# Two graph layers on one core: one exponential over two neighbouring weight tiles in the encoder, and another split of its row sums

## The chip, the cores and the metric

The kernel runs on one core of one Trainium2 chip. The metric is the device time of one execution in microseconds (us). The times below are of whole executions, the profile is of one execution.

## What is computed

The input is `x` (4096 nodes, 512 features) and a 0/1 matrix `adj` of 4096 by 4096. Two layers follow each other: a graph attention autoencoder (encoder attention, a small network, decoder attention with the same weights, a small network), and a second, different graph attention. The change is in the encoder attention alone. Cut to it, the reference is:

```
f1 = einsum('hnd,hd->hn', Xw, V[:, 0]);  f2 = einsum('hnd,hd->hn', Xw, V[:, 1])   # h: 4 heads
sig = sigmoid(f1[:, :, None] + f2[:, None, :])
att = softmax of sig over those j with adj[i, j] != 0, and 0 elsewhere
Xa  = einsum('hij,hjd->hid', att, Xw)
```

A sigmoid is half of a tanh plus a constant, and a constant falls out of a softmax. So the weight of a pair is exp(0.5 · tanh(0.5 · (f1 + f2))) times the mask `adj`; a row's output is the weighted sum of `Xw`, divided by the sum of its weights (the denominator).

## The kernel before, in words

**Blocks and tiles.** `attention` (called for the encoder with the name "enc") goes over eight blocks: four heads, each with two halves of 2048 target nodes. In a block it goes over 32 tiles j of 128 source nodes. A weight tile `e` has 128 partitions (sources) and 2048 columns (targets) of float32, 1 MB. Below, blocks are counted from 1 to 8 and tiles from 0 to 31.

**One tile.** `tanh_weights` makes it: ScalarE takes the tanh of the row `rowb` plus a per-partition score (L571), then the exp in place (L572), and VectorE multiplies by the mask `a` (L573), which SyncE's queue loads from HBM (L213, five buffers). TensorE then multiplies it with the values in four matmuls of 512 columns (L470, for the fourth bank at the block's start L467), into four PSUM banks.

**Denominators.** Each tile must also be added to its block's row sums, in one of three ways. The list `ENC` says how from the fourth block on:

```
ENC = (0, 2, 5, 7, 10, 12, 15, 17, 20, 22, 25), (8, 9, 30, 31)
```

Tiles of the first list are added to `acc2` by transfers: GpSimd's queue issues two per tile, one for each half of the columns, 512 KB each, that add to what is there (L490; the first of a block is a plain copy). Since all of them add to the same tile, each waits for the one before it on its half. Tiles of the second list are multiplied with ones on TensorE (L268). All others are added to `acc` by VectorE (L498, L500). At the end of a block TensorE sums `acc2` and `acc` with ones as well. The first transfer of the next block, which overwrites `acc2`, waits for that.

**Slots.** Weight tiles lie in a ring of eight: `EP` = 2 in the pool `keep`, which the decoder uses too, and 6 in the pool `spool`. Tile j+8 takes the place of tile j, so its tanh waits until everything that reads tile j has ended: the multiply, the matmuls, the transfers of the sum, and for every fifth tile (4, 9, 14, ...) a store to HBM for the decoder (`ekeep`, SyncE's queue, L439).

**A block's ending** runs inside the next block: VectorE copies the banks out (L683) and the denominators (L274), GpSimd's queue sends these to HBM, back as a column (L280), the inverses to HBM (L288), and spread over all partitions (`rb`, L293); VectorE multiplies the output by them (L687) and takes statistics (L690).

**Order.** Each engine works through its own list in order. A scheduler fixes these lists when the program is built, from the order of the code and its own estimates. A wait therefore holds up all that is behind it on its engine. In the lists of before, ScalarE has in the encoder two tanhs, then their two exps, then the next two tanhs.

Of the kernel before, what the change touches and what calls it, by code (L numbers as in the profile page):

```python
# [31 lines left out]
FP = mybir.dt.float32  # L32
U8 = mybir.dt.uint8
AF = mybir.ActivationFunctionType
ALU = mybir.AluOpType
# [4 lines left out]
N, F, H, D, P = 4096, 512, 4, 128, 128  # L40
IB = 512
NIB = N // IB
NJ = N // P
C = IB // P

TB = 2048
NTB = N // TB
SB = TB // IB
# [8 lines left out]
TINY = 1e-30  # L57
# [4 lines left out]
ENC_FIRST = (), (5, 6, 11, 12, 17, 18, 24, 25, 30, 31)  # L62
ENC_SECOND = (12, 14, 17, 19, 22, 24, 26), (1, 2, 4, 5, 7, 8, 30, 31)
ENC_THIRD = (0, 3, 6, 9, 12, 15, 18, 21, 24), (7, 8, 16, 30, 31)
ENC = (0, 2, 5, 7, 10, 12, 15, 17, 20, 22, 25), (8, 9, 30, 31)

GAT_FIRST = (0, 2, 4, 6, 8, 10, 12, 14, 16, 18, 20, 22, 24), (30, 31)
GAT = tuple(range(3, 28, 2)), (31,), True
# [5 lines left out]
EP = 2  # L74

EVICT = 2
INVERT = 4

HB = TB // 2
HD = D // 2  # L80
# [10 lines left out]
def kernel(ctx, tc, x, xT, adjT, w0, w0T, v0, wencT, wdecT, vecs, w1, w1T, a1, outT):  # L91
    nc = tc.nc
# [46 lines left out]
    score = consts.tile([P, 2, NTB, H, NJ // NTB], FP, name="score")  # L139

    def column(t, j, h):
        j = j % (NJ // NTB), j // (NJ // NTB)
        return t[:, j[1], h, j[0]:j[0] + 1]
# [10 lines left out]
    bias = consts.tile([P, C], FP, name="bias")  # L154
# [68 lines left out]

    def attention(what, keep, pools, weights, values, row_of, out, finish, ebufs, modes=None, invert=None,
                  kept=None, sums=None, sums2=None, extras={}, row0=None, masks0=(), in_parts0=1,
                  finish_last=None, behind=(), fast=None):

# [18 lines left out]


        spool, made, masks0 = pools, 0, list(masks0)  # L250
        if invert is not None:
            acc = spool.tile([P, TB], FP, name="acc") if sums is None else sums
            sums2 = (spool.tile([P, TB], FP, name="acc2"), None) if sums2 is None else sums2

        def weight_tile():
            nonlocal made
            made += 1
            if (made - 1) % (EP + ebufs) < EP:
                return keep.tile([P, TB], FP, name="e", tag="ek", bufs=EP)
            return spool.tile([P, TB], FP, name="e", bufs=ebufs)  # L260


        hop = nc.scalar if kept is None else nc.gpsimd
# [129 lines left out]
        later, last_ones, last_main, products_of = {}, None, None, ()  # L393
        rowb = row0 if row0 is not None else next_row_of(0, 0)
        blocks = [(h, tb) for h in range(H) for tb in range(NTB)]
        for n, (h, tb) in enumerate(blocks):
# [14 lines left out]
            for j in range(NJ):  # L411
# [4 lines left out]
                with pinned([a_load, *products_of, last_main] if j else []):  # L416
                    if (n, j) in extras:
                        extras[n, j](a_load)
                    if not last and j == NJ - 10:
                        next_row = next_row_of(*blocks[n + 1])  # L420
                e = weight_tile()
                store = j % KEEP == KEEP - 1 and kept is not None
                if store and kept == "read":
                    a_load = nc.sync.dma_start(e, ekeep[h][tb][j // KEEP])
                else:
                    if masks0:
                        a, a_load = masks0.pop(0)
                    else:
                        a = mask_tile(keep)
                        a_load = load_mask(a, tb, j)  # L430

                    with pinned([*(products_of[:1] if kept == "read" and n == 0 and j < 8 else ()),
                                 *(behind if n == 0 and j < EP else ())]):
                        products_of = weights(e, rowb, a, j, h, SB if NJ * n + j < in_parts0 else 1)


                    if stores and (store if n > 1 else j % KEEP == KEEP - 3):
                        k, t = stores.pop()
                        (nc.sync if n > 1 else nc.scalar).dma_start(ekeep[h][tb][k], t)  # L439
                    if store:  # L440
                        stores.append((j // KEEP, e))
# [3 lines left out]
                elif j - 1 in pairs:  # L445
                    made_sums = sums_second(sums_of, e1, e)
                    products_of = products_of[0], made_sums
# [75 lines left out]
            if not last:  # L523
# [5 lines left out]
                rowb = next_row  # L529
# [39 lines left out]
    def tanh_weights(e, rowb, a, j, h, parts):  # L569
# [3 lines left out]
            last_dve = nc.vector.tensor_mul(e, e, a)  # L573
        return last_act, last_dve

    a_att, b_att, a_mlp, b_mlp = (coefs[:, k, :] for k in range(4))

    with tc.tile_pool(name="keep", bufs=1) as keep:

        with tc.tile_pool(name="f_small", bufs=1) as small, tc.tile_pool(name="f_work", bufs=2) as work:  # L580
            xs = []
# [4 lines left out]
            for ib in range(NIB):  # L586
# [7 lines left out]
                for c in range(0, C, 1 if ib == 0 else C):  # L594
                    n = 1 if ib == 0 else C
# [11 lines left out]
            for ib in range(NIB):  # L607
# [45 lines left out]
                for c in range(C):  # L653
                    j = ib * C + c
# [12 lines left out]
                if ib == SB - 1:  # L667
                    store_rows(rows[0], targets(0))
                    row0 = keep.tile([P, TB], FP, name="rowb", bufs=2)
                    row0_load = load_row(row0, rows[0], 0)  # L670
                    with tc.issue_after(row0_load.ins):
                        masks0 = []
# [48 lines left out]
        with tc.tile_pool(name="enc", bufs=1) as spool:  # L721

            with tc.issue_after(last_copy.ins), tc.issue_after(masks0[-1][1].ins):
                attention("enc", keep, spool, tanh_weights, R[0:4], lambda h, tb: (rows[tb], h), out_enc,
                          (scaled, statistics), 6, lambda n: (ENC_FIRST, ENC_SECOND, ENC_THIRD, ENC)[min(n, 3)],
                          (TINY, ALU.max), "write", row0=row0, masks0=masks0,
                          extras={(2, 8): encoder_weights, (H * NTB - 1, 10): coefs_of_three,
                                  (H * NTB - 1, 12): bias_of_three, (H * NTB - 1, 20): scale_three})

# [43 lines left out]
        with tc.tile_pool(name="m_small", bufs=1) as small, tc.tile_pool(name="m_work", bufs=3) as work:  # L773
# [8 lines left out]
            behind_it = []  # L782
# [54 lines left out]

        with tc.tile_pool(name="dec", bufs=1) as spool:
            attention("dec", keep, spool, tanh_weights, xc, lambda h, tb: (rows[tb], h), out_dec, (scaled, elu), 5,
                      kept="read", behind=behind_it, fast=(z, xd, stationaries),  # L840
                      extras={(H * NTB - 1, 28): decoder_weights})


# [284 lines left out]
```

## Time and profile before

| what | us |
|---|---|
| median of 3 runs (lowest, highest) | 3199.43 (3197.14, 3202.03) |
| the profiled execution, its own time | 3198.86 |
| its span, first to last instruction | 3197.1 |
| one encoder block of 32 tiles (blocks 5, 6, 7) | 118.19, 118.18, 118.19 |
| ScalarE busy in such a block | 118.2 |
| VectorE busy in such a block | 114.3 |
| TensorE busy in such a block | 116.6 |

The profile's busy times are of one execution. A line of a timeline gives the start, the length, the engine, the line of the kernel, what is written and read, how many instructions are taken together, and in brackets how long the engine had been idle and what ended that. Instructions that follow each other directly overlap a little in the records, so a step from start to start is shorter than a length. Matmuls are pipelined and their ends are modelled, so TensorE's busy share overstates its work.

### The profile page before, as it was taken

The page shows a single profiled execution, that of the slowest core. Times are in us where ns is not written, and L with a number is a line of the kernel's source. Part 1 is how long each engine was busy: PE and PEld are TensorE (multiplying, and loading weights), DVE is VectorE, ACT ScalarE, POOL GpSimd, SP SyncE. Part 2 cuts the span into 40 slices and gives each one's busy share as a digit, 9 for nine tenths or more (in the row PEclk, how much of TensorE's full clock was granted, in tenths as well). Part 3 has the DMA queues.
Part 4 walks back from the last instruction along what each step waited for, and adds up shares of the span by engine and source line. Part 5 has one row for each costly group of instructions (what it writes and reads, how often), then busy time and mean ns, then how long its engine had stood idle before and what let it go on. Part 6 is the DMA issues. An engine that isn't in the chain of part 4 may idle for free.

```text
span 3197.1 us, 30054 instructions
## 1 busy us (share of the span) xinstructions
PE 3146.9 (98%) x10539; PEld 1371.7 (43%) x10539; DVE 2938.7 (92%) x2222; ACT 2573.7 (81%) x1825; POOL 525.9 (16%) x680
## 2 busy tenths in 40 slices
PE   7999999999999999999999999999999999999998
PEld 6334444444444463333333333458544444444443
DVE  7989999999999678999999999685699999999998
ACT  7999999999998449999999999466755665666663
POOL 3001211211211000010100100026312222222221
PEclk9999999999999999999999999999999999999999
DMA  9998978988987014444445454322579999899996
GB/s 212 198 194 253 267 209 233 271 223 229 267 227 190 7 44 148 155 159 156 160 162 165 141 168 145 97 105 74 149 193 228 219 219 243 217 213 229 236 213 156
DMA packets 214792, 589.25 MB, mean 184 GB/s; under 512 B 25872, under 2 KB 28976, under 8 KB 198640
## 3 DMA queue, kind: packets, MB, share of 16 engines
q0 software_dynamic: 71008, 231.95, 37.9%
q1 hardware_dynamic: 132200, 332.53, 30.1%
q10 hardware_dynamic: 11432, 22.85, 2.0%
q8 instruction: 83, 1.36, 0.2%
q14 instruction: 69, 0.57, 0.1%
HBM read 378.15 MB, written 84.30 MB: 145 GB/s over the span
## 4 chain that ended last, share of the span: by engine, by line
PE 68%; DVE 15%; issue 8%; ACT 5%; DMA 3%; DVEq 0%; ACTq 0%; POOL 0%; POOLq 0%; SPq 0%
PE ps L470 28%; PE ps L332 22%; PE ps L739 7%; DVE e L573 5%; DVE acc L500 4%; PE den L332 3%; PE ps L950 3%; ACT e L571 3%; DMA a<-mask 3%; DVE R L500 2%; ACT e L572 2%; DVE e L1045 2%; PE den L268 1%; PE ps L799 1%; PE ps L658 1%
## 5 line engine op out<-in xcount | busy, mean ns | idle before, releaser
L470 PE MATMUL ps<-e,R 128*128 128x512 f32 x3992 | 1737.9, 595 | 19.2 <-DVE e L573 16.6
L470 PEld LDWEIGHTS ps<-e,R 128*128 128x128 f32 x3992 | 754.6, 190 | 998.8 <-issue 921.6
L573 DVE TENSOR_TENSOR e<-e,a 128x2048 f32<-128x2048 f32 (+1 forms) x470 | 1049.5, 2261 | 80.2 <-ACT e L572 66.9
L571 ACT ACTIVATE e<-rowb,score 128x2048 f32<-128x2048 f32 (+1 forms) x470 | 909.1, 1969 | 20.3 <-PE ps L332 8.9
L572 ACT ACTIVATE e<-e 128x2048 f32<-128x2048 f32 (+1 forms) x470 | 866.9, 1879 | 4.4 <-DVE e L573 0.7
L332 PE MATMUL ps<-e,R 128*64 128x512 f32 x2624 | 746.8, 592 | 1.6 <-DVE e L573 1.5
L1044 ACT ACTIVATE e<-rowb,nq,jcol 128x2048 f32<-128x2048 f32 x224 | 459.6, 2088 | 263.3 <-DMA w<-e 133.1
L1045 DVE SCALAR_TENSOR_TENSOR e<-e,jcol,a 128x2048 f32<-128x2048 f32 (+1 forms) x265 | 592.9, 2271 | 2.8 <-ACT e L1044 2.8
L332 PEld LDWEIGHTS ps<-e,R 128*64 128x64 f32 x2624 | 241.9, 137 | 319.7 <-issue 316.2
L500 DVE TENSOR_TENSOR R<-R,e 128x2048 f32<-128x2048 f32 x128 | 292.5, 2285 | 0.0
L500 DVE TENSOR_TENSOR acc<-acc,e 128x2048 f32<-128x2048 f32 x122 | 278.7, 2284 | 1.0
L490 POOL DMA_DIRECT2D w<-e x178 | 151.9, 865 | 605.8 <-DMA w<-e 293.1
L739 PE MATMUL ps<-R,w 128*128 128x512 f32 x512 | 220.4, 592 | 0.6 <-DVE w L697 0.6
L490 POOL DMA_DIRECT2D acc<-e x142 | 119.1, 893 | 521.3 <-DMA acc<-e 238.4
L739 PEld LDWEIGHTS ps<-R,w 128*128 128x128 f32 x512 | 97.1, 190 | 123.0 <-issue 117.7
L332 PE MATMUL den<-e,R 128*64 128x512 f32 x320 | 149.8, 592 | 0.0
L332 PE MATMUL ps<-e,w 128*64 128x512 f32 x288 | 138.1, 592 | 0.7 <-DVE e L573 0.7
L293 POOL DMA_DIRECT2D rb<-rinvs x60 | 34.5, 578 | 520.7 <-DVE R L687 449.4
L950 PE MATMUL ps<-w1x,hT 128*128 128x260 f32 x512 | 115.5, 384 | 1.4 <-ACT hT L928 1.4
L332 PE MATMUL ps<-t,w 128*64 128x512 f32 x336 | 111.3, 592 | 1.1 <-DVE t L341 1.1
L950 PEld LDWEIGHTS ps<-w1x,hT 128*128 128x128 f32 x512 | 96.5, 190 | 19.9 <-issue 3.4
L332 PE MATMUL ps<-t,R 128*64 128x512 f32 x192 | 90.2, 592 | 0.0
(209 smaller groups left out, 2115.5 us busy)
## 6 DMA issues: line engine op xcount, KB each, us to landing
a<-mask SPq DMA_DIRECT2D x720, 256.0 KB, 4.3
w<-e POOLq DMA_DIRECT2D x178, 512.0 KB, 6.8
acc<-e POOLq DMA_DIRECT2D x142, 512.0 KB, 7.1
e<-ekeep SPq DMA_DIRECT2D x48, 1024.0 KB, 5.1
ekeep<-e SPq DMA_DIRECT2D x36, 1024.0 KB, 7.1
mask<-in_adjT POOLq DMA_DIRECT2D x8, 2048.0 KB, 105.0
rowb<-rows SPq DMA_DIRECT2D x16, 1024.0 KB, 5.5
rb<-rinvs POOLq DMA_DIRECT2D x60, 256.0 KB, 4.7
```

The costliest lines, as they stand in the source:

```text
L293: hop.dma_start(rb, everywhere(rinvs[h][tb], 0, s * IB, IB))
L332: last_half = nc.tensor.matmul(b[g * HD:(g + 1) * HD, :], weight, x, start=start, stop=stop)
L470: last_main = nc.tensor.matmul(b, block(values[h], j), e[:, s * IB:(s + 1) * IB], start=(j == 0), stop=(j == NJ - 1))
L490: nc.gpsimd.dma_start(into_half, e_half, **({"accum_op": ALU.add} if j > moved[0] else {}))
L500: nc.vector.tensor_add(acc, acc, e)
L571: nc.scalar.activation(e, rowb, AF.Tanh, bias=column(score[:, 1], j, h), scale=0.5)
L572: last_act = nc.scalar.activation(e, e, AF.Exp, scale=0.5)
L573: last_dve = nc.vector.tensor_mul(e, e, a)
L739: last = nc.tensor.matmul(z, w[:, fb, o * P:(o + 1) * P], nodes(src[fb], ib), start=(fb == 0), stop=(fb == C - 1))
L950: m = nc.tensor.matmul(banks[k][:, 0:2 * DX], hT[:, fb, c * P:(c + 1) * P], w1x[:, fb, 2 * k:2 * k + 2, :].rearrange("p h x -> p (h x)"), ...
L1044: last_act = nc.scalar.activation(e, rowb, AF.Relu, bias=column(nq, j, h), scale=column(jcol, j, h))
L1045: last_dve = nc.vector.scalar_tensor_tensor(e, e, column(jcol2, j, h), a, ALU.add, ALU.mult)
```

## The change

From the fourth block on (`PAIRS_FROM = 3`, counted from 0), ScalarE makes two neighbouring tiles with three instructions: two tanhs as before, and one exp over both tiles, 4096 columns. For that the two tiles must lie side by side, so the ring's slots become slices of two persistent tiles (`ring` with 2 slots, `er` with 6). The decoder takes its two shared slots from the same `ring`. The multiply by the mask stays one instruction per tile, and both multiplies of a pair now need the pair's exp.

The list of the row sums changes as well: twelve tiles instead of eleven go by transfers, three instead of four by ones; VectorE's share stays at 17 tiles.

```diff
-ENC = (0, 2, 5, 7, 10, 12, 15, 17, 20, 22, 25), (8, 9, 30, 31)
+ENC = (0, 2, 4, 6, 8, 10, 13, 15, 17, 20, 22, 24), (12, 30, 31)
...
+PAIRS_FROM = 3
...
+        ring2 = spool.tile([P, ebufs, TB], FP, name="er") if by_pairs is not None else None
...
+        def slots_of_two():
+            nonlocal made
+            k = made % (EP + ebufs)
+            made += 2
+            return ring[:, k:k + 2, :] if k < EP else ring2[:, k - EP:k - EP + 2, :]
...
-                e = weight_tile()
+                by_two = by_pairs is not None and n >= PAIRS_FROM
+                if not by_two:
+                    e = weight_tile()
+                elif j % 2:
+                    e = two[:, 1, :]
+                else:
+                    two = slots_of_two()
+                    e = two[:, 0, :]
...
-                        products_of = weights(e, rowb, a, j, h, SB if NJ * n + j < in_parts0 else 1)
+                        if not by_two:
+                            products_of = weights(e, rowb, a, j, h, SB if NJ * n + j < in_parts0 else 1)
+                        else:
+                            if j % 2 == 0:
+                                last_act = by_pairs(two, rowb, j, h)
+                            products_of = last_act, nc.vector.tensor_mul(e, e, a)
...
+    def tanh_pairs(two, rowb, j, h):
+        for k in range(2):
+            nc.scalar.activation(two[:, k, :], rowb, AF.Tanh, bias=column(score[:, 1], j + k, h), scale=0.5)
+        both = two.rearrange("p k i -> p (k i)")
+        return nc.scalar.activation(both, both, AF.Exp, scale=0.5)
...
+        ring = keep.tile([P, EP, TB], FP, name="ek")
```

What the scheduler makes of it, read from the lists of both programs: ScalarE's list from the fourth block on is tanh 2k+1, tanh 2k+2, exp of the pair (2k, 2k+1), tanh 2k+3, tanh 2k+4, and so on. The tanh of the next pair's first tile thus stands ahead of the exp. Once in each of the blocks 5 to 8, at the pair of tiles 6 and 7, and at the last pair of block 8, the exp comes directly behind its own second tanh. On GpSimd's queue the order from a block's start is: transfers of tiles 0, 2, the denominators out and back, transfers of tiles 4, 6, 8, the inverses out, transfer of tile 10, three of the four spreads `rb`, then tile 13 and on (in blocks 4 and 8 the first spread stands ahead of tile 10). Before it was 0, 2, denominators, 5, 7, inverses, three spreads, 10, 12 and on. SyncE's list is unchanged in the encoder, and the rest of the program keeps its order but for a few neighbours.

More of the change, by code (lines that the diff above doesn't have):

```diff
@@ L225, in attention @@
                   kept=None, sums=None, sums2=None, extras={}, row0=None, masks0=(), in_parts0=1,
-                  finish_last=None, behind=(), fast=None):
+                  finish_last=None, behind=(), fast=None, ring=None, by_pairs=None):
         spool, made, masks0 = pools, 0, list(masks0)
+        ring2 = spool.tile([P, ebufs, TB], FP, name="er") if by_pairs is not None else None
         if invert is not None:
@@ L257, in weight_tile @@
             made += 1
-            if (made - 1) % (EP + ebufs) < EP:
-                return keep.tile([P, TB], FP, name="e", tag="ek", bufs=EP)
-            return spool.tile([P, TB], FP, name="e", bufs=ebufs)
+            k = (made - 1) % (EP + ebufs)
+            if k < EP:
+                return ring[:, k, :] if ring is not None else keep.tile([P, TB], FP, name="e", tag="ek", bufs=EP)
+            return ring2[:, k - EP, :] if by_pairs is not None else spool.tile([P, TB], FP, name="e", bufs=ebufs)
+        def slots_of_two():
[3 more added lines that the diff above has]
+            return ring[:, k:k + 2, :] if k < EP else ring2[:, k - EP:k - EP + 2, :]
         hop = nc.scalar if kept is None else nc.gpsimd
@@ L725 @@
                           (scaled, statistics), 6, lambda n: (ENC_FIRST, ENC_SECOND, ENC_THIRD, ENC)[min(n, 3)],
-                          (TINY, ALU.max), "write", row0=row0, masks0=masks0,
+                          (TINY, ALU.max), "write", row0=row0, masks0=masks0, ring=ring, by_pairs=tanh_pairs,
                           extras={(2, 8): encoder_weights, (H * NTB - 1, 10): coefs_of_three,
@@ L839 @@
             attention("dec", keep, spool, tanh_weights, xc, lambda h, tb: (rows[tb], h), out_dec, (scaled, elu), 5,
-                      kept="read", behind=behind_it, fast=(z, xd, stationaries),
+                      kept="read", behind=behind_it, ring=ring, fast=(z, xd, stationaries),
                       extras={(H * NTB - 1, 28): decoder_weights})
```

## The prediction

> **What bounds the kernel now.** I read the busy time of each engine block by block first: the change touches encoder blocks 4 to 8 alone, and a share over the whole span mixes stages. Blocks 5 to 7:
>
> ```profile
> 550.05:668.24 118.19, 116.56 (x304) 49.50 (x304) 114.34 (x64) 118.19 (x65) 22.29 (x29) 1.00 0.89 240
> 668.24:786.42 118.18, 116.56 (x305) 49.50 (x305) 114.34 (x64) 118.18 (x65) 22.41 (x29) 1.00 0.90 240
> 786.42:904.61 118.19, 116.57 (x305) 49.50 (x305) 114.34 (x64) 118.19 (x65) 22.34 (x29) 1.00 0.92 249
> ```
>
> The columns are stretch, length, busy PE, weight loads, DVE, ACT, POOL, clock, DMA share, GB/s. ACT is busy in the whole block; DVE lacks 3.8 us, PE 1.6. DMA runs at 0.90. The chain of waits names PE first, but a matmul's wait lists several semaphores and PE's own work is shorter: 64 matmul records of eight tiles take 27.47 us without a pause, so 32 tiles take 109.9, and six sums with ones at 0.87 add 5.2: 115.1.
>
> ACT's timeline shows the pace:
>
> ```profile
> 785.02 3.88 ACT L571 ACTIVATE e<-rowb,score 128x2048 f32<-128x2048 f32 x2
> 788.81 3.69 ACT L572 ACTIVATE e<-e 128x2048 f32<-128x2048 f32 x2
> 792.41 3.88 ACT L571 ACTIVATE e<-rowb,score 128x2048 f32<-128x2048 f32 x2
> ```
>
> Two tiles take 792.41 - 785.02 = 7.39 us: two tanhs 3.79 and two exps 3.60. 16 such pairs are 118.2, the block. ACT never waits for a slot here. What the change needs of the slots is shown by GpSimd's queue in block 7:
>
> ```profile
> 793.13 1.09 POOL L490 DMA_DIRECT2D acc<-e  x2 [27.35 <-PE den L268]
> 796.54 0.87 POOL L490 DMA_DIRECT2D acc<-e  x1 [2.31 <-DMA acc<-e]
> 798.02 0.85 POOL L490 DMA_DIRECT2D acc<-e  x1 [0.62 <-DMA acc<-e]
> 798.57 0.87 POOL L275 DMA_DIRECT2D dens<-dsb  x1
> 805.59 0.58 POOL L280 DMA_DIRECT2D dcol<-dens  x1 [6.16 <-DMA dens<-dsb]
> 806.16 1.81 POOL L490 DMA_DIRECT2D acc<-e  x2
> 812.29 0.85 POOL L490 DMA_DIRECT2D acc<-e  x1 [4.32 <-DMA acc<-e]
> 815.47 0.85 POOL L490 DMA_DIRECT2D acc<-e  x1 [2.32 <-DMA acc<-e]
> ```
>
> Tile 0's transfer is released by the previous block's sums on PE; tile 2 follows half by half; tile 5 waits behind the denominators' round trip until 13.0 us after tile 0; tile 7's halves are released by tile 5's landings at 19.2 and 22.3. So a tile's transfer holds its half for some 6 to 9 us and the next waits. The transfers' load from 550 to 1020 us:
>
> ```profile
> acc<-e POOLq DMA_DIRECT2D x88, 512.0 KB, 6.9
> q0 software_dynamic: 14336, 50.44, 52.8%
> q1 hardware_dynamic: 22392, 62.81, 37.0%
> ```
>
> A half lands 6.9 us after its issue (median); the two queues together fill 89.8%.
>
> **Two rules of the skill.** "ScalarE: Activation LUTs", section "What ACT_TABLE_LOAD costs": an ACTIVATE without a pointer operand costs 186 ns plus 0.833 ns a column, and neighbours overlap by 93 ns. The trace agrees: the exps of 512 and 2048 columns
>
> ```profile
> L572 ACT ACTIVATE e<-e 128x2048 f32<-128x2048 f32 x163 | 301.4, 1896 | 0.0
> L572 ACT ACTIVATE e<-e 128x512 f32<-128x512 f32 x4 | 2.3, 614 | 0.0
> ```
>
> give (1896 - 614) / 1536 = 0.835 ns a column and 0.19 us fixed, and 1.80 from start to start says that 0.09 of it is left. I go by the trace. "DMA: Bandwidth & Descriptors", section "Queues, rings and completion order": an engine takes turns between the queues that have work for it. So one more accumulate slows masks and stores in turn; the 89.8% above is the room for it.
>
> **The change part by part.**
>
> *Merged exp.* An exp of 4096 columns takes 1.80 + 2048 x 0.835 = 3.51 us from start to start against 3.60: 0.09 saved. At worst nothing (3.60); more than 0.18 is excluded, since the columns alone take 3.42. 16 pairs save 1.5: ACT alone would need 116.7 us. Where an exp stands directly behind its own tanh (once in blocks 5 to 8 each, once more in block 8) it waits for the tanh's end: at the decoder's start such a step took 2.02 us against 1.89, so 0.13 x 5 = 0.6 in all.
>
> *Sums.* One tile less by ones takes 0.87 off PE (114.2), which lies under ACT. DVE keeps its 114.3. One tile more by transfers adds two issues of 0.85 on GpSimd's queue (22 of 118 us busy) and DMA time: 0.528 x 470 us / 44 tiles, less the small ones, is some 5.5 us a tile; 0.898 x 118.2 + 5.5 = 111.6 of 116.7, 96%.
>
> *Later multiplies.* Before, a pair's first multiply could start 1.8 us before the second exp ended. Now both wait for the pair's exp. In mid-block DVE does wait for exps:
>
> ```profile
> 724.25 2.29 DVE L573 TENSOR_TENSOR e<-e,a 128x2048 f32<-128x2048 f32 x1 [0.69 <-ACT e L572]
> ```
>
> That is tile 16 of block 6, and behind it DVE is busy up to the block's end. So DVE's chain to the end, PE's closing sums and tile 0's transfer of the next block all come 1.8 us later against ACT.
>
> *Earlier slots.* Tanh 2k+2 now stands ahead of exp k, 5.4 us (1.89 + 3.51) earlier against the exps than before. If its slot isn't free, exp k waits behind it, though its input is ready; behind that wait tiles 2k and 2k+1 on DVE, their matmuls and their transfers. The transfers lie mostly on even tiles. How much there is to lose, in block 7:
>
> ```profile
> 837.17 0.85 POOL L490 DMA_DIRECT2D acc<-e  x1 [2.03 <-DMA acc<-e]
> 844.11 3.88 ACT L571 ACTIVATE e<-rowb,score 128x2048 f32<-128x2048 f32 x2
> ```
>
> The first is tile 12's second half, released by tile 10's landing at 836.9; the second, counted from the block's first tanh, is tile 18's, which takes tile 10's slot: 7.2 us to spare. Against it stand 5.4 + 1.8, and 0.3 to 1.5 for ACT's faster pace. The cover is gone. Tiles 13, 15 and 17 lie on second slots, whose tanh stays behind an exp; they lose 1.9 + 1.8 of their 3.5 to 8 us and are not first.
>
> *The loop.* Tile 16's multiply at 724.25 to tile 0's transfer at 793.13 is 68.9 us, unchanged. From there: tile 4 takes tile 5's place and lands at +22.3; tanh 12 waits for it; from tanh 12 to the end of its exp is 1.89 + 3.61 = 5.5, then three pairs of 7.30: 68.9 + 22.3 + 27.4 = 118.6. Further: tile 6's second half is issued at 22.3, lands at 29.2; tile 8 at 36.4; tile 10 at 43.6, or some 46 if the spreads beside it slow it (tile 10 of before took 10 us beside them). Then tanh 18 and its exp, 5.5: 68.9 + 43.6 to 46 + 5.5 = 118.0 to 120.4. I take 119.0. The loop and not ACT sets a block then: +0.8, in blocks 5 to 8 +3.2. In block 4 the block before it is still made tile by tile and doesn't bring the 1.8; tile 10 had 5.9 us to spare there against 5.4 + 0.8, and has one transfer more ahead of it, some 1.4. So a loss of about what the exps save: 0.
>
> *The inverses* go out behind tile 8 and the spreads behind tile 10. They are needed behind tile 16's multiply, about +49; issued at 37 they land by 44 (4.7 to 6.9). Covered; if not, DVE waits.
>
> *End of the encoder.* Tiles 30 and 31 are multiplied one after the other from the last exp's end: 1017.03 + 4.49 = 1021.5 against 1020.38 now, +1.1, and PE, den and the small network follow it.
>
> Sum: +3.2 + 1.1 = +4.3 on the profiled 3198.86 (span 3197.1), so 3203.2. The median of the runs is 0.6 above that execution: 3203.7.
>
> **Rivals.** *ACT stays the bound.* If the transfers land some 2 us earlier than I count, no tanh waits: -7.4 (5 x 1.49) + 0.6 + 1.1 = -5.7, 3193.7. For it: the next layer's attention issues 13 transfers a block. Against it: the slacks above. With 0.14 saved a pair instead of 0.09 it would be 3190. Chance 0.25.
>
> *The DMA engines saturate.* In block 7 they are near it already, with 1.07 and 1.03 in the DMA column here:
>
> ```profile
> 803.00:813.00 10.00, 10.00 (x24) 4.37 (x23) 10.00 (x5) 10.00 (x7) 3.08 (x4) 1.00 1.07 282
> 813.00:823.00 10.00, 10.00 (x25) 4.46 (x24) 8.05 (x7) 10.00 (x6) 1.58 (x3) 1.00 1.03 282
> ```
>
>  If the transfers of tiles 4 to 10 follow each other every 8.5 us, as tiles 10 to 22 do now (836.9 to 880.2, five tiles), tile 10 lands at 12 + 4 x 8.6 + 1 = 47.5 and a block takes 121.9: 4 x 3.7 + 1.1 = +16, 3215. It decides from a landing later than about +45. Against it: tile 7 landed 6.8 after tile 5. Chance 0.2.
>
> *The exp of 4096 columns costs what two cost.* Then nothing is saved and the loop gives the same 119 with 0.1 more. It moves little, and is in the forecast's range.
>
> **Numbers.** About 0.2% (6.4 us) is what a measurement of this kernel can tell from no change. The forecast, chance 0.5, reaches from -2 to +10: of it 0.28 within 0.2%, 0.21 slower, 0.01 faster. ACT as the bound: 0.14 faster, 0.11 the same, since -5.7 lies beside the limit. Saturation: slower, 0.2. Of 0.05 unseen, 0.03 is faster, 0.01 each the rest. Together 0.18 faster, 0.40 the same, 0.42 slower. The range, 3190 to 3217, goes from the first rival's best to a little beyond the second's middle.
>
> **What would show it.** ACT's timeline: an exp of 4096 columns 3.6 us long, 3.51 from start to start. ACT's idle time, zero now, must show 2 to 3 us a block before a tanh, released by DMA acc<-e, at tiles 12 to 18. Blocks of 119 us. I am wrong if blocks take 116.7 with ACT never idle, if idle time on ACT is released by others, or if DVE waits for masks or spreads.

## The result, and the profile after

The changed kernel takes 3218.05 us (median of 5 runs, 3216.57 to 3219.92) against 3199.43 (also 5 runs): ratio 1.0061, 95% interval 1.0050 to 1.0071. It is slower, by 18.6 us where 4.3 was forecast, and 1 us above the range's end. The profiled spans, 3216.2 and 3197.1, differ by 19.1. Where that arises, read at marks in both traces:

| mark | shift against before, us | added since the mark above |
|---|---|---|
| last multiply of block 3 | -0.4 | |
| last multiply of block 4 | +7.4 | +7.8 |
| of block 5, 6, 7 | +8.6, +10.6, +13.8 | +1.2, +2.0, +3.3 |
| of block 8 | +14.5 | +0.65 |
| first matmul of the small network | +16.3 | +1.8 |
| end of the decoder's attention | +20.7 | +4.4 |
| last instruction | +19.1 | -1.6 |

The windows of the changed kernel for blocks 4 to 8, from tile 31's multiply to the next block's (columns as in the prediction's first fence):

```profile
431.70:557.40 125.70, 118.79 (x301) 49.46 (x299) 114.67 (x64) 117.80 (x49) 24.20 (x31) 1.00 0.89 234
557.40:676.77 119.37, 116.16 (x296) 49.11 (x296) 114.54 (x65) 118.39 (x50) 23.98 (x31) 1.00 0.91 247
676.77:796.91 120.14, 116.16 (x296) 49.06 (x296) 114.38 (x65) 116.73 (x49) 23.98 (x31) 1.00 0.91 245
796.91:918.38 121.47, 116.43 (x296) 49.01 (x296) 114.39 (x65) 117.15 (x49) 23.99 (x31) 1.00 0.93 251
918.38:1034.85 116.47, 113.61 (x306) 49.92 (x307) 107.97 (x72) 114.50 (x56) 24.19 (x31) 0.99 0.92 240
```

ACT was busy in the whole of a block before. Now it lacks 7.9 us in block 4 and 1.0 to 4.3 in blocks 5 to 7; VectorE is still at 114.4. So ScalarE is no longer the bound, and no other engine has taken its place. ScalarE's waits in the encoder (operation, line, releaser, total, times, longest) say what did; before, the same list had none of these (two smaller ones, 1.4 and 0.7 us, behind TensorE and VectorE are left out):

```profile
ACT er L602 <- DMA acc<-er: 9.8, 8, 3.1
ACT ek L602 <- DMA acc<-ek: 6.2, 6, 2.0
```

All are tanhs (L602) whose slot isn't free, nearly all because a transfer of a sum still reads it. The largest are in block 4, in ScalarE's timeline:

```profile
483.25 1.99 ACT L602 ACTIVATE ek<-rowb,score 128x2048 f32<-128x2048 f32 x1
488.31 2.00 ACT L602 ACTIVATE er<-rowb,score 128x2048 f32<-128x2048 f32 x1 [3.08 <-DMA acc<-er]
490.22 3.60 ACT L604 ACTIVATE ek<-ek 128x4096 f32<-128x4096 f32 x1
493.73 3.88 ACT L602 ACTIVATE er<-rowb,score 128x2048 f32<-128x2048 f32 x2
...
510.02 2.00 ACT L602 ACTIVATE er<-rowb,score 128x2048 f32<-128x2048 f32 x1 [1.61 <-DMA acc<-er]
...
519.47 2.00 ACT L602 ACTIVATE ek<-rowb,score 128x2048 f32<-128x2048 f32 x1 [2.04 <-DMA acc<-ek]
```

At 488.31 tile 18's tanh starts 0.1 us after tile 10's second half has landed (488.21). The exp of tiles 16 and 17 stands behind it and starts at 490.22, although its second tanh ended at 485.24: this is the step "Earlier slots", seen word for word. The tanhs at 510.02 and 519.47 are those of tiles 23 and 25, released by tiles 15 and 17. From 490.22 to 493.73 the merged exp takes 3.51, and all of them are 3.6 long:

```profile
L604 ACT ACTIVATE er<-er 128x4096 f32<-128x4096 f32 x60 | 216.2, 3603 | 0.1
```

Why tile 10 landed so late in block 4 is in GpSimd's queue:

```profile
466.37 0.84 POOL L513 DMA_DIRECT2D acc<-ek  x1 [2.74 <-DMA acc<-er]
469.27 0.85 POOL L513 DMA_DIRECT2D acc<-ek  x1 [2.06 <-DMA acc<-er]
470.46 0.59 POOL L299 DMA_DIRECT2D rinvs<-dcol  x1 [0.33 <-issue]
478.40 0.56 POOL L304 DMA_DIRECT2D rb<-rinvs  x1 [7.35 <-DMA rinvs<-dcol]
478.95 1.83 POOL L513 DMA_DIRECT2D acc<-er  x2
```

Tile 8's halves (issued 466.37 and 469.27) landed at 474.58 and 477.73, and tile 10's could have followed. Ahead of them stands the first spread of the inverses (L304), which waits for the inverses' write (L299), landing at 478.1. Tile 10 goes out at 478.95, its first half 4.4 us late, its second 1.8. Block 5 has no spread there, and tile 10's first half is issued 0.5 us after tile 8's landed (598.6):

```profile
592.32 0.86 POOL L513 DMA_DIRECT2D acc<-ek  x1 [1.39 <-DMA acc<-er]
...
599.11 0.84 POOL L513 DMA_DIRECT2D acc<-er  x1 [5.37 <-DMA acc<-ek]
```

ScalarE's account: 80 pairs save 0.0925 each, -7.4; waits of the tanhs, summed from start to start over what they take undisturbed, +20.3 (by block 8.4, 1.0, 3.5, 3.9, 3.4; in before none); exps directly behind their own tanh, once in each of blocks 5 to 8, +0.5; a short tanh of the decoder that now stands ahead of the last exp, +0.6; ScalarE's earlier start into block 4 (421.63 against 423.07), -1.4. That is +12.6. The last exp ends at 1029.97 against 1017.03, +12.9; the rest lies in steps that are each under 0.1 us too long. Of the 20.3, 13.4 fall on first tiles of pairs (0, 12, 16, 18, 28) and 6.9 on tiles 23 and 25.

### The profile page after: what moved, and what is told of

Same layout as the page of the kernel before. It is cut to its first block, busy times and chain, and to the rows that moved or that the text cites. A ratio compares the mean times of both kernels' runs of the same rounds, so it can differ in the third digit from the quotient of the medians.

```text
span 3216.2 us, 29883 instructions
## 1 busy us (share of the span) xinstructions
PE 3143.4 (98%) x10499; PEld 1542.7 (48%) x10499; DVE 2939.6 (91%) x2222; ACT 2568.9 (80%) x1745; POOL 529.1 (16%) x690
## 4 chain that ended last, share of the span: by engine, by line
PE 41%; DVE 27%; issue 15%; DMA 11%; ACT 4%; POOL 1%; DVEq 0%; ACTq 0%; POOLq 0%; SPq 0%
PE ps L343 23%; DVE e L1076 8%; DVE R L523 7%; PE ps L770 7%; DMA acc<-er 4%; DMA a<-mask 4%; DVE acc L523 3%; PE ps L981 3%; PE den L343 3%; DMA w<-e 2%; PE ps L493 2%; DVE er L596 2%; DVE er L457 2%; DVE ek L457 1%; DVE ek L596 1%
## 5 line engine op out<-in xcount | busy, mean ns | idle before, releaser
L493 PE MATMUL ps<-e,R 128*128 128x512 f32 x1984 | 857.5, 593 | 1.9 <-DVE e L1076 1.8
L493 PE MATMUL ps<-er,R 128*128 128x512 f32 x1528 | 674.4, 597 | 28.7 <-DVE er L457 18.3
L493 PEld LDWEIGHTS ps<-e,R 128*128 128x128 f32 x1984 | 375.6, 190 | 482.8 <-issue 463.8
L343 PE MATMUL ps<-e,R 128*64 128x512 f32 x1872 | 489.4, 593 | 3.3 <-DVE e L596 3.3
L493 PEld LDWEIGHTS ps<-er,R 128*128 128x128 f32 x1528 | 287.9, 191 | 410.2 <-issue 345.3
L596 DVE TENSOR_TENSOR e<-e,a 128x2048 f32<-128x2048 f32 x148 | 336.0, 2289 | 37.8 <-ACT e L595 37.2
L594 ACT ACTIVATE e<-rowb,score 128x2048 f32<-128x2048 f32 x148 | 292.7, 1994 | 15.1 <-PE ps L343 9.0
L457 DVE TENSOR_TENSOR er<-er,a 128x2048 f32<-128x2048 f32 x120 | 270.5, 2283 | 26.5 <-ACT er L604 26.5
L595 ACT ACTIVATE e<-e 128x2048 f32<-128x2048 f32 x148 | 280.0, 1907 | 2.3
L602 ACT ACTIVATE er<-rowb,score 128x2048 f32<-128x2048 f32 x120 | 235.2, 1989 | 10.0 <-DMA acc<-er 9.8
L596 DVE TENSOR_TENSOR ek<-ek,a 128x2048 f32<-128x2048 f32 (+1 forms) x90 | 193.2, 2156 | 17.8 <-ACT ek L595 14.1
```

What stands on the lines that cost most here:

```text
L343: last_half = nc.tensor.matmul(b[g * HD:(g + 1) * HD, :], weight, x, start=start, stop=stop)
L457: products_of = last_act, nc.vector.tensor_mul(e, e, a)
L493: last_main = nc.tensor.matmul(b, block(values[h], j), e[:, s * IB:(s + 1) * IB], start=(j == 0), stop=(j == NJ - 1))
L594: nc.scalar.activation(e, rowb, AF.Tanh, bias=column(score[:, 1], j, h), scale=0.5)
L595: last_act = nc.scalar.activation(e, e, AF.Exp, scale=0.5)
L602: nc.scalar.activation(two[:, k, :], rowb, AF.Tanh, bias=column(score[:, 1], j + k, h), scale=0.5)
```

## The experiments

Encoder means the shift of the small network's first matmul in the profile against before, decoder what is added by the decoder's end. Ratios are to the kernel before on the same chip. ten_slots and half_transfers leave out part of the computation, so only their times count.

| run | median us | ratio, 95% interval | encoder | decoder |
|---|---|---|---|---|
| changed kernel | 3218.05 | 1.0061, 1.0050 to 1.0071 | +16.3 | +4.4 |
| list_only | 3201.66 | 1.0010, 1.0004 to 1.0017 | +2.6 | 0 |
| pairs_old_list | 3206.65 | 1.0025, 1.0013 to 1.0036 | +3.75 | +4.1 |
| ring_only | 3202.75 | 1.0012, 1.0005 to 1.0018 | -0.1 | +4.7 |
| ten_slots | 3200.65 | 1.0006, 0.9998 to 1.0015 | -3.8 | +4.4 |
| dec_pool | 3217.25 | 1.0060, 1.0046 to 1.0073 | +19.6 | 0 |
| odd_dec_pool | 3202.21 | 1.0011, 1.0005 to 1.0018 | +2.95 | 0 |
| pinned | 3217.50 | 1.0061, 1.0045 to 1.0076 | +17.0 | +4.4 |
| from5 | 3221.02 | 1.0071, 1.0057 to 1.0085 | +17.7 | +4.4 |
| half_transfers | 3201.27 | 1.0008, 1.0000 to 1.0017 | -1.3 | +5.6 |
| ten_odd | 3195.60 | 0.9991, 0.9983 to 0.9999 | -1.8 | 0 |
| spread_later | 3215.77 | 1.0053, 1.0041 to 1.0066 | +14.1 | +4.4 |
| spread_later_own_pool | 3209.50 | 1.0034, 1.0022 to 1.0046 | +12.8 | 0 |

**One half of the change at a time.** list_only is the kernel before with the new `ENC`; pairs_old_list is the changed kernel with the old one; ring_only has the old list and the ring, but no pairs.

```diff
-PAIRS_FROM = 3
+PAIRS_FROM = 99     # ring_only, with the old ENC
```

> The kernel before with the new list (twelve by transfers, three by ones) and nothing else. Slot theory (the loss comes from tanhs that ask for their slots 5.4 us earlier and multiplies that come 1.8 us later): the transfers keep some 7 us to spare, ScalarE never waits, blocks stay at 118.2, 3199 +- 3 us. Load rival (the twelfth transfer alone saturates the DMA engines): ScalarE waits for landings here as well, blocks of 119 to 121, 3207 to 3215.

> The changed kernel with the old list (eleven by transfers, four by ones). Slot theory: the lead and the later multiplies stay, but tiles 5, 7, 15, 17 and 25 lie on second slots; ScalarE waits for tiles 10, 12, 20 and 22, 1 to 2 us a block; encoder +3 to +8 and the decoder's +4.4, 3207 to 3212. Load rival: ScalarE never waits, the encoder gains 5, the decoder loses 4.4: 3199. Coupling rival (what costs is that both multiplies of a pair wait for one exp, not the slots): as in the changed kernel, 3215 or more.

> The changed kernel's persistent ring with the old list, and no tile made by pairs (PAIRS_FROM = 99). All three theories: the encoder as before, 118.2 a block. If the decoder's +4.4 us comes from the order that the scheduler makes of ring slices: 3203.8, with that loss in the decoder's first block. If it comes from the encoder's lateness: 3199.4.

Neither half is dear: +2.6 and +3.75 in the encoder, where both together give +16.3. Only with both do the slots run short in every block. In list_only ScalarE waits twice, both times at tile 25 (2.4 in block 4, 1.2 in block 6): it keeps the order tanh, tanh, exp, exp, and twelve transfers alone fit nearly. So the twelfth transfer's load by itself is not the cause. In pairs_old_list the waits are 7.8 us in four places, at tiles 18 and 20 of blocks 4, 7 and 8.

ring_only, without a pair and with the old list, loses nothing in the encoder (one wait of 1.2 us, at tile 25 of block 4, does not show at the block's end) and 4.7 in the decoder. What differs there is the order on ScalarE. Its timeline at the decoder's start, and VectorE's (below the dots), the first fence from before, the second from ring_only:

```profile
1181.94 1.91 ACT L572 ACTIVATE e<-e 128x2048 f32<-128x2048 f32 x1
1183.76 1.99 ACT L571 ACTIVATE e<-rowb,score 128x2048 f32<-128x2048 f32 x1
1185.78 1.91 ACT L572 ACTIVATE e<-e 128x2048 f32<-128x2048 f32 x1
...
1187.72 2.29 DVE L573 TENSOR_TENSOR e<-e,a 128x2048 f32<-128x2048 f32 x1 [1.54 <-ACT e L572]
```

```profile
1181.87 1.91 ACT L595 ACTIVATE e<-e 128x2048 f32<-128x2048 f32 x1
1183.68 1.99 ACT L594 ACTIVATE e<-rowb,score 128x2048 f32<-128x2048 f32 x1
1185.58 1.99 ACT L594 ACTIVATE ek<-rowb,score 128x2048 f32<-128x2048 f32 x1
1187.47 1.89 ACT L595 ACTIVATE e<-e 128x2048 f32<-128x2048 f32 x1
...
1189.39 2.29 DVE L596 TENSOR_TENSOR e<-e,a 128x2048 f32<-128x2048 f32 x1 [3.29 <-ACT e L595]
```

Before, the first tiles of the decoder are made one by one. With its two shared slots as slices of one tile, the scheduler puts the third tile's tanh (`ek`) ahead of the second's exp, and VectorE, which has nothing else to do there, waits 3.29 us instead of 1.54. The order of the first dozen tiles stays different, and 4.1 to 4.7 us, 5.6 in half_transfers, are never made good.

**More slots.** ten_slots gives the ring a fifth pair of slots:

```diff
-            k = made % (EP + ebufs)
+            k = (made - PAIRS_FROM * NJ) % (EP + ebufs + 2)
...
+            if k == EP + ebufs:
+                return R[4].rearrange("p (k i) -> p k i", k=2)
```

> The changed kernel with a fifth pair of slots from the fourth block on. It lies where the first head's output is, which is overwritten: this leaves the first head's output out. Transfers, list and pairs as in the changed kernel, 7.3 us more for each slot. Slot theory: ScalarE never waits for a landing, blocks of 116.7 to 117, the encoder gains some 5 us, the decoder still loses 4.4: 3198 to 3200. Load rival and coupling rival: blocks stay at 119 to 121, 3214 to 3218.

The waits are nearly gone: 1.4 us in two places are left of 20.3, and the encoder is 3.8 faster than before. The transfers are as slow as ever, with a spread ahead of tile 10 in block 4 too and that tile landing at 488.5 (488.2 in the changed kernel). So the coupled multiplies, VectorE and TensorE do not cost this time by themselves; a late transfer costs nothing unless a tanh needs its slot. This run carries the main conclusion.

**The early tanh or the chain of transfers?** pinned holds each pair's first tanh behind the exp before it, so that no tanh takes its slot early:

```diff
+        with pinned(last_exp):
             for k in range(2):
                 nc.scalar.activation(two[:, k, :], rowb, AF.Tanh, ...)
...
+        last_exp[:] = [nc.scalar.activation(both, both, AF.Exp, scale=0.5)]
```

> The changed kernel with each pair's first tanh held behind the exp of the pair before, so that ScalarE goes tanh, tanh, exp, and no slot is asked for early. Each exp then stands directly behind its own tanh: 0.13 us more a pair against 0.09 saved, 7.43 us a pair, 118.9 a block. Slot theory: transfers have 5.4 us more, ScalarE waits for landings for at most 1 us a block; encoder +4 to +8, decoder +4.6, 3208 to 3212. If the later multiplies and the DMA load matter and the lead does not: landings late as in the changed kernel, blocks of 120 to 121, 3218 or more.

By its time alone this run tells nothing: a new cost takes the place of what is saved. Every exp now stands directly behind its own tanh; a pair takes 7.43 us where it took 7.30, some 10 us over 80 pairs:

```profile
562.09 3.88 ACT L605 ACTIVATE er<-rowb,score 128x2048 f32<-128x2048 f32 x2
...
569.52 3.88 ACT L605 ACTIVATE er<-rowb,score 128x2048 f32<-128x2048 f32 x2
```

The waits tell more. Those at tiles 12, 16 and 18 are gone; those at 23 and 25 stay, and 21 joins them. These are the places of the transferred tiles 13, 15 and 17. In block 4:

```profile
500.34 2.00 ACT L605 ACTIVATE er<-rowb,score 128x2048 f32<-128x2048 f32 x1 [2.29 <-DMA acc<-er]
...
509.31 2.00 ACT L605 ACTIVATE er<-rowb,score 128x2048 f32<-128x2048 f32 x1 [1.42 <-DMA acc<-er]
...
519.35 2.00 ACT L605 ACTIVATE ek<-rowb,score 128x2048 f32<-128x2048 f32 x1 [2.49 <-DMA acc<-ek]
```

At these three tiles 11.4 us of waits remain, against 6.9 in the changed kernel; 2.7 more are at the decoder's first tanh, near the end of block 8. So there are two causes: the early tanh, for the even tiles 4, 8 and 10 (though ScalarE's slower pace in pinned helps them too), and the chain of transfers itself, which by tiles 13 to 17 is behind even without it. Two runs with no early tanh and no slower pace agree on the second: list_only waits at tile 25, and from5 (below) waits 4.6 us at tiles 21, 23 and 25 of block 4, which it still makes tile by tile. The kernel before was close to it. In its block 4 the second half of tile 17 has landed just before tile 20's second half goes out at 512.75, and tile 25's tanh, the second of the pair below, starts at 513.59, 1.1 us after the landing (first GpSimd's queue, then ScalarE):

```profile
512.75 0.86 POOL L490 DMA_DIRECT2D acc<-e  x1 [4.14 <-DMA acc<-e]
511.70 3.89 ACT L571 ACTIVATE e<-rowb,score 128x2048 f32<-128x2048 f32 x2
```

odd_dec_pool goes at the first cause in another way. It moves the transfers to second tiles of pairs (eleven of them), whose tanh doesn't come early, and gives the decoder its slots from a pool of its own; dec_pool does only the latter.

```diff
-ENC = (0, 2, 4, 6, 8, 10, 13, 15, 17, 20, 22, 24), (12, 30, 31)
+ENC = (1, 3, 5, 7, 11, 13, 15, 17, 21, 23, 25), (8, 9, 30, 31)     # odd_dec_pool
...
-        ring = keep.tile([P, EP, TB], FP, name="ek")
+        ring = ring_pool.enter_context(tc.tile_pool(name="rk", bufs=1)).tile([P, EP, TB], FP, name="ek")
...
+        ring_pool.close()       # before the decoder, which then opens a pool there
```

> Pairs, the decoder's own pool, and eleven tiles by transfers that all lie on second slots (1, 3, 5, 7, 11, 13, 15, 17, 21, 23, 25; by ones 8, 9, 30, 31). A second slot's tanh stays behind an exp, so it loses 3.7 of its 7 to 9 us and not 7.2. Slot theory: ScalarE waits for no landing or for less than 0.5 us a block, blocks of 116.8 to 117.3, encoder -3 to -5, 3194 to 3197. Load rival: as with the old list, ScalarE waits some 2 us a block, 3202.

> The changed kernel, but the decoder takes its two slots from a pool of its own at the place of the ring, tile by tile, as before the change. ScalarE's list in the decoder is then that of before. If the decoder's loss is the order that the scheduler made of ring slices: 4.6 us less than the changed kernel, 3213 to 3214, the encoder still 16 us late. If it is the slots' memory or the encoder's lateness: 3218.

In both the decoder's order and time are those of before: its +4.4 is 0. dec_pool's total hardly moved all the same (3212.56 to 3221.36 over four runs), since in its profile the encoder lost 19.6 instead of 16.3, with the same lists there. Whether the pool or chance did that isn't shown: in another pair of runs below, which differ by the pool in the same way, the encoder is 1.3 faster with it. A gain of 4 us is not read from dec_pool's median. odd_dec_pool waits only at tiles 23 and 25, again the places of 15 and 17 (2.1 us in block 4, 4.2 in block 6). It missed its 3194 to 3197 by about these.

**Which blocks pay.** Block 4 lost 7.8 us, the others 0.7 to 3.3. from5 starts the pairs one block later.

```diff
-PAIRS_FROM = 3
+PAIRS_FROM = 4
```

> The changed kernel with pairs from the fifth block on (PAIRS_FROM = 4), the new list from the fourth as before. Block 4 lost 7.8 us in the changed kernel, 1.8 of it the one shift of the multiplies. Slot theory: block 4 is back at some 118.5, block 5 takes the shift and 1 to 3 us; 4 to 6 us less than the changed kernel, 3212 to 3214. If the first block of pairs always costs 7.8: block 5 takes it all, 3217.

Block 5 now lost 10 us and block 4 only 1.5. So the first block of pairs pays. A part of that is plain: its last multiply is later once, since both multiplies of a pair wait for the pair's exp. Where ScalarE waits for nothing in block 4, in half_transfers and ten_odd (below), its last multiply still loses 1.75 and 1.85. A second candidate is in GpSimd's queue: in from5 it is block 5, not 4, that has the spread ahead of tile 10, and tile 10 lands there 11.1 us after tile 8. spread_later takes only this away:

```diff
+            with tc.issue_after(tenth.ins) if kept == "write" and tenth is not None else nullcontext():
                 hop.dma_start(rb, everywhere(rinvs[h][tb], 0, s * IB, IB))
```

Here `tenth` is tile 10's second transfer. Of all lists, only that of GpSimd's queue changes, in blocks 4 and 8.

> The changed kernel with one difference in its lists: in blocks 4 and 8 the first spread of the inverses stands behind tile 10's transfer on GpSimd's queue, as in the other blocks. There the spread waited for the inverses' landing (478.1) and tile 10's first half went out at 479.0, 4.4 us after tile 8's first half had landed (474.6); its second half landed 10.5 us after tile 8's, in blocks 5 to 7 it was 6.9 to 8.5. The same order stood in block 5, not 4, of the kernel with pairs from the fifth block on, and there block 5 paid. If this order is why block 4 loses most, tile 18's waits (3.2 in block 4, 2.0 in block 8) go, tile 10 lands some 8 us behind tile 8, and the encoder ends about 5 us earlier: 3213. If the chain's density alone is the cause, tile 18 waits as before or the wait moves to tiles 23 and 25, and the time stays at 3217 to 3218.

> The run before with the decoder's two slots from a pool of its own as well, which restores the order of the decoder's first block. If the loss of the changed kernel is the sum of the two places (spread ahead of a transfer some 5 us, decoder's order 4.4) and of the rest of the waits, the encoder ends as in the run before and the decoder adds nothing: 3218.0 - 5 - 4.4 = 3208 to 3209. What is then left against 3199 is the twelve transfers' chain. If the encoder's waits only change from run to run, both runs scatter between 3210 and 3218 whatever the order.

GpSimd's queue and, below the dots, ScalarE's timeline of spread_later in block 4:

```profile
469.52 0.86 POOL L514 DMA_DIRECT2D acc<-ek  x1 [2.12 <-DMA acc<-er]
...
475.27 0.85 POOL L514 DMA_DIRECT2D acc<-er  x1 [3.98 <-DVE acc L526]
478.16 0.86 POOL L514 DMA_DIRECT2D acc<-er  x1 [2.04 <-DMA acc<-ek]
478.69 1.99 POOL L305 DMA_DIRECT2D rb<-rinvs  x3
...
485.50 2.00 ACT L605 ACTIVATE er<-rowb,score 128x2048 f32<-128x2048 f32 x1
...
506.68 2.00 ACT L605 ACTIVATE er<-rowb,score 128x2048 f32<-128x2048 f32 x1 [1.07 <-DMA acc<-er]
...
516.89 2.00 ACT L605 ACTIVATE ek<-rowb,score 128x2048 f32<-128x2048 f32 x1 [2.81 <-DMA acc<-ek]
```

Tile 10 goes out at 475.27 and lands 7.5 us behind tile 8, not 10.5. Tile 18's wait falls from 3.2 to 0.2 in block 4 and from 2.0 to 0 in block 8. With the own pool it falls too, from 3.4 in dec_pool to 1.3, and from 2.3 to 0. But tile 25 and block 6 wait longer than in the changed kernel (+0.8 and +2.4), so that the encoder gains 2.2 us and not 5. Block 4 loses 5.0 instead of 7.8 (with the own pool 4.5 instead of 7.5), still more than any other block. The two medians, 3215.77 and 3218.05, differ by as much, and their intervals overlap; with the own pool the pair is 3209.5 against 3217.25, and the intervals only touch. The place of the spread is shown as the cause of most of the wait at tile 18 in blocks 4 and 8, and of some 3 of block 4's 7.8 us. What it is worth in the end lies between 2 and 8 us.

**The chain itself.** half_transfers leaves out six of the twelve transfers; ten_odd is odd_dec_pool with tile 15 summed by ones.

```diff
+                    if by_pairs is not None and n >= PAIRS_FROM and j in (2, 6, 10, 15, 20, 24):
+                        pass
-                    if j in moved:
+                    elif j in moved:
```

> The changed kernel, but from the fourth block on the transfers of tiles 2, 6, 10, 15, 20 and 24 are left out, so that those six tiles miss in the row sums (left out of the computation). Order of ScalarE, pairs, ring and decoder as in the changed kernel. Two things are to be read. First, if ScalarE's waits come from transfers that follow each other too closely in one chain, none is left in blocks 4 to 8 and the encoder ends 16.3 + 3.8 = 20 us earlier than in the changed kernel, as with ten slots: about 3198. If waits of about 3 us a block remain at tiles 12, 16 and 18, it is the early tanh against a single transfer's own length, not the chain: about 3210. Second, the length of one transfer from issue to landing: if the engines' load makes them slow, a 512 KB half takes clearly less than 6.9 us here, 4 to 5 us; if 6.9 is its own length, it stays.

> A version meant to be faster than both: pairs, the decoder's slots from its own pool, and ten tiles by transfers (1, 3, 5, 7, 11, 13, 17, 21, 23, 25), all of them second tiles of their pairs, five by ones (8, 9, 15, 30, 31). Against the run with eleven such transfers the one of tile 15 goes to ones, 0.87 us more on TensorE a block (116.0 of some 116.8). There the waits at tiles 23 and 25 cost 6.3 us in all and the encoder ended 2.95 late. If the chain's density is the cause, those waits go and the encoder ends 3 us early: 3195 to 3197 against 3198.5. If TensorE at 116 becomes the bound, blocks take 117.5 to 118.5 without waits for transfers, and the time is 3199 to 3202.

In half_transfers one wait of 0.5 to 0.7 us is left in each of blocks 5 to 8, at tile 12. Tile 4's transfer goes out there 0.3 us behind its own multiply, with no transfer ahead of it, and takes some 11 us. That is the early tanh without the chain, 2.4 us in all. The encoder is 17.6 faster than in the changed kernel (20 were expected). The DMA lines from 550 to 1020 us, the first fence of the changed kernel, the second of half_transfers (queues: packets, MB, share of 16 engines; issues: median from issue to landing):

```profile
q0 software_dynamic: 15200, 53.58, 55.2%
q1 hardware_dynamic: 21829, 61.52, 36.0%
acc<-er POOLq DMA_DIRECT2D x64, 512.0 KB, 6.9
a<-mask SPq DMA_DIRECT2D x124, 256.0 KB, 4.8
```

```profile
q1 hardware_dynamic: 22608, 63.19, 38.8%
q0 software_dynamic: 8576, 29.46, 28.9%
a<-mask SPq DMA_DIRECT2D x129, 256.0 KB, 3.0
acc<-ek POOLq DMA_DIRECT2D x24, 512.0 KB, 4.9
acc<-er POOLq DMA_DIRECT2D x24, 512.0 KB, 7.2
```

The engines' share falls from 91% to 68% and masks land in 3.0 instead of 4.8 us. A tile's transfer hardly gets shorter. The two medians mix first and second halves; by GpSimd's timeline both halves of a tile are now issued together, and for most tiles the first lands some 5 us later, the second 7 to 8 (tile 13 of block 4: issued at 481.1 and 481.6, landed at 485.5 and 488.6, 7.5 for both). The exceptions are tile 4, 10.7 to 11.3 for both halves, and tiles 8 and 13 of block 7, 10.9 and 9.9. In the changed kernel, from tile 4's landing to tile 24's, a new tile lands every 8.3 to 8.9 us in the mean of a block. So neither of the two expectations for the length holds: a tile takes 7.2 to 8.5 us with the engines at 68%, and in the full chain about 1 more. What it takes on idle engines no run shows. The chain isn't full as a whole: from tile 0's issue to tile 24's landing it takes 97 to 102 us of a block. It falls behind in places. ScalarE makes two tiles in 7.3 us, the seven from tile 10 to tile 17 in 25.6. Between their landings the chain takes 31.1, 29.1, 28.8 and 27.9 us in blocks 4 to 7, and these blocks wait at tiles 23 and 25; in block 8 it takes 23.4, and they don't wait there.

With ten transfers on second tiles, ten_odd has no wait for a slot in blocks 4 to 8; blocks 6 and 7:

```profile
669.65:786.65 117.00, 117.00 (x313) 49.82 (x312) 114.07 (x65) 116.94 (x49) 20.74 (x27) 1.00 0.87 234
786.65:903.63 116.98, 116.98 (x313) 49.82 (x312) 114.07 (x65) 116.92 (x49) 20.70 (x27) 1.00 0.88 243
```

Blocks of 117.0: ScalarE's own 116.7 and 0.3 for exps behind their tanhs. TensorE is busy throughout by its records too, which overstate it; ScalarE's steps there show no wait for it. The pairs' gain is there when nothing stands in its way, 1.2 us a block. Block 4 and the encoder's end take part of it back, 1.8 is left (the program's end adds another 1.9 in the profile, not explained), and 3195.6 against 3198.7 is the best of all versions, though by less than the 0.2% named in the prediction.

## Why the prediction was wrong, step by step

The direction and the mechanism were right: a tanh that asks for its slot too early, and transfers that hold it. Three terms of the sum failed. Block 4 was put at 0 and took 7.8 us; the decoder was put at nothing, without a reason, and took 4.4; blocks 5 to 8 were put at 3.2 and took 7.1.

- **Merged exp: right.** 3.51 from start to start, 116.7 a block for ScalarE alone (117.0 measured without waits), 0.13 for an exp behind its own tanh (pinned). The Trainium skill's rule ("ScalarE: Activation LUTs", section "What ACT_TABLE_LOAD costs") gives 186 + 4096 x 0.833 = 3598 ns; the trace has 3603.
- **Sums: right in load, and not what decides.** The DMA share was to be 96% of a block of 116.7, some 112 us; it is 0.91 of 119.4 to 0.93 of 121.5, 109 to 113. What decides is that the transfers follow one another.
- **Earlier slots: right in mechanism and place for tiles 12, 16 and 18; too narrow.** "Tiles 13, 15 and 17 lie on second slots ... and are not first" failed: their slots' next tanhs, at 21, 23 and 25, wait in pinned without any early tanh, and 23 and 25 took 3.8 of block 4's 8.4 us and 6.9 of the 20.3 in all. By the prediction's own figures 3.5 us less 1.9 + 1.8 was already no cover, and in block 4 of before, which its 3.5 to 8 leave out, tile 17 had 1.1 and tile 15 3.3 us to spare.
- **The loop: near in its sum, too narrow in what waits.** The term that was too small is tile 10's landing after tile 0's issue, put at 43.6 to 46. Measured, it is 44.1, 45.4 and 46.9 in blocks 5, 6 and 7, which with its 68.9 and 5.5 gives 118.5, 119.8 and 121.3; the blocks took 119.4, 120.1 and 121.5. Tile 8 is where it slips: it lands 9.0 to 9.2 behind tile 6, not 7.2. But the three terms make up a block whatever holds it back, so the agreement proves little: in blocks 5 and 6 tile 18 itself doesn't wait, and 12, 16, 23 and 25 do. Blocks 5 to 8 cost 7.1 where 3.2 was taken.
- **Block 4: "0" failed, and is the largest miss.** It lost 7.8. Some 1.8 of it is the later last multiply (1.75 and 1.85 in the two runs without waits in block 4), which the prediction counts only at the encoder's end. Some 3 are the spread ahead of tile 10 (7.8 against 5.0, 7.5 against 4.5). "The change" names it for blocks 4 and 8, but the prediction puts the spreads behind tile 10 everywhere and gives this no price. Tile 10's landing there is 48.0 and 49.4 after tile 0's issue: on GpSimd's queue the 512 KB transfer took over the wait of the spread ahead of it. The differences are of one profile each. What is left are waits that stay with the spread out of the way: 5.6 us in block 4 of spread_later, 4.1 of them at tiles 23 and 25, and 2.7 with the own pool, at tiles 12, 16 and 18.
- **The inverses: right** as far as VectorE goes; it waited for no spread. The cost went to the transfer behind instead.
- **End of the encoder: 1.1 was 3.4.** From the last exp (+12.9) to the last multiply another 1.5 is lost (the shift that the marks show in block 4 already), since VectorE does its last six multiplies in one row; TensorE waits for the first of these and then has 40 matmuls before it, which adds 1.8:

```profile
1023.90 17.43 PE L493 MATMUL ps<-er,R 128*128 128x512 f32 x40 [1.26 <-DVE er L457]
```

- **The decoder was not in the sum.** Its order on ScalarE had changed ("The change" says "but for a few neighbours"), and it cost 4.4. It was in the lists, to be read beforehand.

Together: 12.9 + 3.4 + 4.4 - 1.6 = 19.1. The -1.6 at the program's end is not explained.

Of the rivals, "The DMA engines saturate" came nearest in time (3215, with "decides from a landing later than about +45"), but that is partly luck: it takes 3.7 for each of blocks 5 to 8 and nothing for block 4 and the decoder, where 1.2, 2.0, 3.3 and 0.65, 7.8 and 4.4 were measured. Its reason is half right: the engines are at 0.91, and with them at 0.68 a tile still takes 7.2 to 8.5 us. "ACT stays the bound" is what ten_slots and ten_odd show when slots suffice. The Trainium skill's "DMA: Bandwidth & Descriptors", section "Queues, rings and completion order", was used for the room left on the engines; that masks land in 3.0 instead of 4.8 us with half the transfers gone agrees with its taking turns, but no run here shows the turns themselves.

Open: why blocks differ by up to 2 us in their waits with the same lists, why the encoder loses 16.3 in one profile and 19.6 in another with the same lists, why tile 4's transfer takes 11 us in half_transfers, and why the order of the decoder's first tiles is never made good.

## What to carry to other kernels

A faster engine gains only if its buffers come free in time: write down for each buffer the last reader's landing and the next writer's start, ahead of and behind the change, and price every instruction in the queue that issues the last reader. A chain of accumulating transfers has a pace of its own (8.3 to 8.9 us a tile here), so where its links come faster than that, the list must leave gaps in which it catches up. With pairs, going from the eleven transfers of the old list to the twelve of the new, closer together, cost the encoder 12.5 us (3.75 against 16.3), more than the 7.4 that the merged exps save. When a buffer becomes a slice of a larger tile, compare the order of everything else that uses it, stages later too.

## What the runs showed that was not expected

- A 1 MB tile added by two accumulating transfers mostly takes 7.2 to 8.5 us for both halves even with the DMA engines at 68%. The fit in the Trainium skill's "DMA: Bandwidth & Descriptors", section "Anatomy of one DMA — SWDGE (gpsimd) path", 2.0 us plus bytes over 436 GB/s, would give an estimate of 3.2 for a half and 4.4 for both together; it doesn't reckon with other traffic, and the measurement decides.
- One spread of 256 KB ahead of a transfer held its first half for 4.4 us, not by the spread's own 0.56 us of issue but by its wait for another write.
- Without a pair made, a ring in place of separate slots cost 4.7 us, in another stage than the one that was changed.
